# Seven products for the first token block's second projection, sums begun in the fifth half unit, last norm six half units later

## The chip, the cores and the metric

The kernel runs on one core of a Trainium2 chip. The metric is the device time of one execution in microseconds, lower is better; for the kernel before it is the median of three runs. The core has a matrix engine (PE, with its weight loads shown as PEld), three engines for elementwise work (DVE, ACT, POOL) and a queue that issues most DMAs (SP). Each engine works through its own queue in order, and waits for others by semaphores.

## What is computed

One transformer layer on 2 sequences of 1024 tokens with 256 features: self attention with 16 heads, cross attention to 154 context rows, and a gated feed-forward layer, each behind a layer norm and added to its input. All is fp32. The change lies in the last part:

```python
h = _layernorm(x, ln3_g, ln3_b)
p = h @ ff_w1 + ff_b1                      # 256 -> 2048
a, gate = (p[..., :D_FF], p[..., D_FF:])   # 1024 each
h = a * jax.nn.gelu(gate, approximate=False) @ ff_w2 + ff_b2   # 1024 -> 256
return h + x
```

## The kernel before

The program order of each engine is the order of the Python code (`tc.manual_schedule`). There are three stages: a loop over self attention, a loop over cross attention (variable `c`), and the last loop over half units (`k` from 0 to 63), which holds the gated layer. The change touches the last loop alone.

**Token blocks and units.** The 2048 tokens are cut into four blocks (`pair` 0 to 3) of 512 tokens, two halves of 256 each. Each block goes through eight units `n`, one for each slice of 128 of the 1024 hidden features. A unit has two half units: `gate_first(n)` at k = 2n and `gate_second(n)` at k = 2n + 1. The first projection is done in the manner of Strassen and Winograd: seven products of 256 columns in place of eight, with sums of weights and of tokens prepared by POOL (`weight_sums`, `token_sums`) and sums of results taken by DVE. An even half unit has four products on PE, since `gate_last(n - 1)` puts the seventh of the unit before in its middle; an odd one has three. POOL multiplies the two halves by their gates: L1081 (second half, emitted in the odd half unit) and L1090 (first half, emitted in the even half unit after, by `gate_last`). The results are the tiles `u`; the second half of block 0 lies in the old tile `kT`.

**Second projection.** When `gate_last` has done a block's last unit, it puts that block's products into the list `sums`, and the loop takes them from there by `sum_slot`, so block 0's products run beside block 1's units, from k = 16 on. Blocks 1 to 3 go through `partial`: seven products for each of two token halves, each of four matrix products with 128 columns, into the tiles `pf` (L1161). The seven need sums of weights (`column_sums`, four POOL instructions of 128x512, L1128, once) and sums of the gated values (`row_sums`, four POOL instructions of 128x256 for each of four pairs of slices, L1140 to L1143). `store` adds the results to `x` on DVE (L1170), five additions for each token half, and sends the finished token tiles on SP. Block 0 does the plain form: eight matrix products of 256 columns for each of four token tiles (L1200), one addition each (L1210), two products in every half unit.

**What else stands in the loop.** The last cross attention values are weighed at k = 0 and k = 3 (`poc`, L932), and the four last output pieces of cross attention (`py_ca`, L467) run at k = 4 to 6. At k = 7 `norm_beside("ff", B - 1)` queues the norm of the second sequence: from there each odd half unit runs one of seven steps, which together hold the statistics of two tiles on DVE (L240, L241), variance and power of the pair before on POOL (L246, L250), the factor `off` on DVE (L256) and the normalization of the pair before that on POOL (L267), then the transposes on PE (L280) and the scaling on ACT (L295). Token sums for the next block come at k = 8, 24, 40. From k = 13 on every third half unit lets POOL add the output bias to one token tile of `x` (L320); a DVE addition to the same tile that comes later in the program waits for it. `hold_sums` takes the buffer for column and row sums at k = 16; it is one of two buffers with the tag `pT`, and the one it takes held the transposed probabilities of cross attention until k = 3.

In the engines' queues the tile `own` of a unit holds its four intermediate results; DVE's L1060, L1062 and ACT's L1056 start a unit, L1076, L1079 and L1088 on DVE and L1074, L1080 on ACT finish it. PE's second product into a tile `pb` waits until L1060 has read the first.

Of the kernel before, what the change touches and what calls it, by code (L numbers as in the profile page):

```python
# [10 lines left out]
ALU = mybir.AluOpType  # L11
AX = mybir.AxisListType

P = 128
# [4 lines left out]
def tile_transformer_block(ctx: ExitStack, tc: tile.TileContext, a: dict, out: bass.AP):  # L19
    nc = tc.nc  # L20
# [3 lines left out]
    B, S, D = x.shape  # L24
# [7 lines left out]
    NT = S // P  # L32
    GT = 4
# [17 lines left out]
    NF = DF // P  # L51
    SH = GH // 2
    TF = 2
# [19 lines left out]
    def sum_tile(name):  # L73

        return ps_o.tile([P, HB], F32, tag="po", name=name)


    xt = {
        (b, g): const.tile([P, GT, D], F32, tag=f"x{b}{g}", name=f"x{b}{g}")
        for b in range(B) for g in range(NG)  # L80
    }
# [16 lines left out]
    for n in names:  # L98
        k = n_of[n]
# [8 lines left out]
    for n in names[:2]:  # L108
        for r0 in range(0, P, HR):
            (nc.scalar if n == names[0] else nc.sync).dma_start(  # L110
                out=cols[r0:r0 + HR, row_of[n]:row_of[n] + NH],
                in_=w[n].rearrange("(r p) -> p r", p=HR),
# [54 lines left out]
    for n in names[2:]:  # L167
        own = rows[row_of[n] - n_cols:row_of[n] - n_cols + n_of[n], :]
# [396 lines left out]
    def flush(queue):  # L565
        for fn in queue:
            fn()
        queue.clear()
# [188 lines left out]
    CG = [(t, min(TG, NT - t)) for t in range(0, NT, TG)]  # L757
# [204 lines left out]
    NPR = B * 2  # L962
    BT = S // 4
    FU = NPR * NF
    wsum, wh, ub, psum, pools = {}, {}, {}, {}, {}
# [98 lines left out]
    def biases(n):  # L1064
        c = row_of["ff_b1"] + n % NF
        return cols[:, c:c + 1], cols[:, c + NF:c + NF + 1]
# [16 lines left out]
    def gate_last(n):  # L1083

        pair, f = divmod(n, NF)
        pa, pb, pc, own = psum.pop(n)
        product(n, 4, pb, False)
        nc.vector.scalar_tensor_tensor(  # L1088
            own[:, 0, :], pb[:, :BT], biases(n)[0], own[:, 0, :], op0=ALU.add, op1=ALU.add)
        nc.gpsimd.tensor_tensor(ub[pair][0][:, f, :], own[:, 0, :], own[:, 3, :], ALU.mult)  # L1090
        if f == NF - 1:
            if pair:
                early, late = (1, 4, 2), (5, 6, 3, 7)
                if pair == NPR - 1:
                    sums.extend((pair, i, m) for m in early for i in range(TF))
                    sums.extend((pair, i, m) for i in range(TF) for m in late)
                else:
                    sums.extend((pair, i, m) for i in range(TF) for m in early + late)
            else:
                sums.extend((pair, i, e) for i in range(2 * TF) for e in range(NF))  # L1100

    sums, summed = [], {}

# [18 lines left out]
    def quarter(odd, d):  # L1122
        return w2[:, odd::2, d * P:(d + 1) * P]

    def column_sums(n):

        t = half["t"]
        nc.gpsimd.tensor_tensor(*[  # L1128
            lambda: (t[5], quarter(0, 1), quarter(0, 0)),
            lambda: (t[6], quarter(1, 1), t[5]),  # L1130
            lambda: (t[4], quarter(1, 0), t[6]),
            lambda: (t[7], quarter(1, 1), quarter(0, 1)),
        ][n](), ALU.subtract)

    def row_sums(pair, c):

        s = {i: own[:, c, :] for i, own in half["s"][pair % 2].items()}
        (a11, a12), (a21, a22) = ([ub[pair][j][:, 2 * c + e, :] for e in range(2)] for j in range(2))
        tt = nc.gpsimd.tensor_tensor
        tt(s[5], a21, a22, ALU.add)  # L1140
        tt(s[6], s[5], a11, ALU.subtract)
        tt(s[3], a12, s[6], ALU.subtract)
        tt(a21, a11, a21, ALU.subtract)  # L1143

    def partial(pair, i, m):

        if m == 1:
            bank = mm_tile if pair == NPR - 1 and i else sum_tile
            summed[pair, i] = [bank(f"pf{pair}_{i}_{r}") for r in range(2)]
        into, own = summed[pair, i]  # L1150
        at = {2: 0, 3: 1, 4: 2, 5: 3}.get(m)
        region = own[:, (m != 1) * P:][:, :P] if at is None else into[:, at * P:(at + 1) * P]
        token = slice(i * P, (i + 1) * P)
        for c in range(NF // 2):
            lhs = {
                1: lambda: ub[pair][0][:, 2 * c, token], 2: lambda: ub[pair][0][:, 2 * c + 1, token],
                4: lambda: ub[pair][1][:, 2 * c + 1, token], 7: lambda: ub[pair][1][:, 2 * c, token],
            }.get(m, lambda: half["s"][pair % 2][m][:, c, token])()
            rhs = {1: (0, 0), 2: (1, 0), 3: (1, 1)}.get(m)
            rhs = half["t"][m][:, c, :] if rhs is None else quarter(*rhs)[:, c, :]  # L1160
            nc.tensor.matmul(  # L1161
                region, lhsT=lhs, rhs=rhs, start=(c == 0 and m != 7), stop=(c == NF // 2 - 1),
                skip_group_check=True)
        if m in (2, 4, 5):
            return None
        b, g = divmod(pair, NG)
        xs = xt[b, g].rearrange("p (j i) (d k) -> p i j d k", i=TF, k=P)[:, i]

        def plus(x, y):
            nc.vector.tensor_tensor(x, y, x, ALU.add)  # L1170

        def send(j, queue):
            t = 2 * TF * pair % NT + j * TF + i
            queue.dma_start(out=out[b, t * P:(t + 1) * P, :], in_=xt[b, g][:, j * TF + i, :])

        def store():
            if m == 1:
                plus(xs, region.unsqueeze(1).unsqueeze(1).broadcast_to([P, 2, 2, P]))
            elif m == 6:
                plus(xs[:, 0, 1], region)  # L1180
            elif m == 3:
                plus(xs, into.rearrange("p (j d k) -> p j d k", j=2, d=2))
                plus(xs[:, 0, 1], into[:, 3 * P:4 * P])
                send(0, nc.sync)
            else:
                plus(xs[:, 1], region.unsqueeze(1).broadcast_to([P, 2, P]))
                send(1, nc.scalar if pair == NPR - 1 and i else nc.sync)

        return store

    def sum_slot():

        pair, i, f = sums.pop(0)
        if pair:
            return partial(pair, i, f)
        if f == 0:
            summed[pair] = sum_tile(f"pf{pair}_{i}")
        own = summed[pair]
        j, e = divmod(i, TF)
        nc.tensor.matmul(  # L1200
            own[:, :D], lhsT=ub[pair][j][:, f, e * P:(e + 1) * P], rhs=w2[:, f, :],
            start=(f == 0), stop=(f == NF - 1),
        )
        if f < NF - 1:
            return None
        b, t = divmod(pair * 2 * TF + i, NT)

        def store():
            xs = xt[b, t // GT][:, t % GT, :]
            nc.vector.tensor_tensor(xs, own[:, :D], xs, ALU.add)  # L1210
            nc.sync.dma_start(out=out[b, t * P:(t + 1) * P, :], in_=xs)

        return store


    with tc.manual_schedule():
# [11 lines left out]
        own = [ps_s.tile([P, 2, HB], F32, tag="s", name=f"first_{r}") for r in range(2)]  # L1228
# [88 lines left out]
        for c in range(CA):  # L1317
# [5 lines left out]
            if c == SH:  # L1323
                out_pieces("sa", B - 1, NQ - 1, out_order("sa"))
                w1, w2, parts = hold_gated()
# [27 lines left out]
            if n == 0 and ui > 1:  # L1353
                own, between = cross_values(ui - 2, [mm_tile] * 2 + [sum_tile] * 2)
# [54 lines left out]
        for k in range(2 * FU):  # L1409
            c = CA + k  # L1410
            weighed = {0: [part_tile] * 3 + [sum_tile], 3: [part_tile] * 2 + [sum_tile] * 2}.get(k)
            flush(adds)
            if k == 0:
                for copies in cross_values(NU - 2, weighed):
                    copies()
            (gate_second if k % 2 else gate_first)(k // 2)
            flush(stores)
            flush(lates)
            if k == 2 * len(CG) + 1:
                norm_beside("ff", B - 1)  # L1420
            if k == 0:
                load_out("ca", B - 1, NQ - 1)
            cross_drain(c)
            if k == len(CG):
                for copies in cross_values(NU - 1, weighed):
                    copies()
                out_pieces("ca", B - 1, NQ - 1, out_order("ca"))
            if k % (2 * NF) == NF and k < 2 * FU - 2 * NF:
                token_sums(k // (2 * NF) + 1)
            for _ in range(min(2 if k < 4 * NF else 1, len(sums))):  # L1430
                run(sum_slot)
            flush(stores)
            run_work(0 if k <= len(CG) else 1 + k % 2, k % 2)
            if later and k > 12 and k % 3 == 1:
                later.pop(0)()
            if k == 2 * NF:
                hold_sums()
            if k in (2 * NF + 2, 2 * NF + 4, 2 * NF + 8, 2 * NF + 10):
                column_sums((k - 2 * NF) // 3)
            pair, at = divmod(k - 5, 2 * NF)  # L1440
            if pair > 0 and at % 4 == 0:
                row_sums(pair, at // 4)
# [38 lines left out]
```

## Time and profile before

| | us |
|---|---|
| median of three runs | 1078.48 (1077.67 to 1078.64) |
| profiled execution, its own time | 1078.65 |
| span of that execution | 1076.9 |
| POOL busy over the span | 765.4 |
| DVE busy over the span | 875.2 |

The span is what the trace of the profiled execution covers; 1.75 us of its time lie around it. Rows of a timeline give start and length in us, engine, line, operation, output and inputs, the number of instructions merged, and in brackets the idle time ahead of it with what ended it. Rows of windows give the busy time of each engine in a stretch.

### The profile page before, as it was taken

Reading aid. Unit: us, or ns where it says so; the run is one execution under the profiler, and the core shown is the slowest. Engines: PE = TensorE matmul, PEld = TensorE weight load, DVE = VectorE, ACT = ScalarE, POOL = GpSimd, SP = SyncE. Lnnn points to the kernel's source line nnn. Section 1 sums busy time; section 2 is a strip of 40 time slices with the busy share of each in tenths; the row PEclk is TensorE's granted clock in tenths of the full one; section 3 lists DMA queues with packets and bytes.
Section 4 is the critical chain, followed back from the end, with each engine's and each line's share of the span. In section 5 each row is a group of like instructions: output and inputs, shape, how many; then the busy total and the mean of one; then the engine's idle time right before and its main releaser. Section 6 shows DMA issues by size and latency. Waiting matters only on the chain.

```text
span 1076.9 us, 45967 instructions
## 1 busy us (share of the span) xinstructions
PE 1065.6 (99%) x19060; PEld 712.3 (66%) x19060; DVE 875.2 (81%) x1283; ACT 651.0 (60%) x2081; POOL 765.4 (71%) x1600
## 2 busy tenths in 40 slices
PE   8999999999999999999999999999999999999998
PEld 6545657567565565566665655567766677788998
DVE  5789999998989989999989998978766777654554
ACT  5666767667666666666776666666566555242221
POOL 2677777778777787777777777768665687488774
PEclk9999999999999999999999999999999999999999
DMA  3232122111111111211211211135323221000000
GB/s 95 63 91 63 46 47 46 33 43 30 41 40 33 43 43 29 53 43 24 53 24 33 53 24 38 24 103 131 97 57 83 68 58 41 1 10 11 21 11 30
DMA packets 99234, 50.56 MB, mean 47 GB/s; under 512 B 30218, under 2 KB 97810, under 8 KB 99026
## 3 DMA queue, kind: packets, MB, share of 16 engines
q1 hardware_dynamic: 97698, 46.96, 18.0%
q8 instruction: 150, 2.46, 1.0%
q10 hardware_dynamic: 1328, 0.66, 0.2%
q14 instruction: 58, 0.48, 0.1%
HBM read 35.25 MB, written 3.41 MB: 36 GB/s over the span
## 4 chain that ended last, share of the span: by engine, by line
PE 91%; POOL 3%; DVE 2%; DMA 1%; ACT 1%; issue 1%; SPq 1%; DVEq 0%; POOLq 0%; ACTq 0%
PE s L493 19%; PE po L547 19%; PE py_sa L467 5%; PE py_ca L467 5%; PE pv_sa L393 5%; PE pq_ca L362 5%; PE pq_sa L362 5%; PE pk_sa L362 5%; PE sc L867 4%; PE poc L932 4%; PE pb L1037 3%; PE pf L1161 3%; PE pa L1037 2%; PE pc L1037 2%; PE pf L1200 1%; DMA st<-st 1%
## 5 line engine op out<-in xcount | busy, mean ns | idle before, releaser
L613 POOL TENSOR_SCALAR p<-p,rd,ee 128x512 f32<-128x512 f32 x508 | 387.4, 773 | 91.4 <-DVE rd L605 88.1
L508 ACT ACTIVATE p<-s,st 128x512 f32<-128x512 f32 x512 | 345.9, 687 | 175.5 <-DVE st L502 169.7
L502 DVE TENSOR_REDUCE st<-s 128x2 f32<-128x1024 f32 x256 | 308.8, 1207 | 51.1 <-issue 20.4
L640 DVE STREAM_TRANSPOSE pT<-p 128x1024 f32<-128x1024 f32 x256 | 302.4, 1219 | 1.5 <-POOL p L613 1.5
L493 PE MATMUL s<-k_sa,q_sa 64*32 64x512 f32 x4096 | 256.1, 591 | 2.4 <-ACT p L508 1.6
L547 PE MATMUL po<-pT,v_sa 64*32 64x256 f32 x8192 | 239.5, 376 | 0.9 <-ACT p L885 0.9
L547 PEld LDWEIGHTS po<-pT,v_sa 64*32 64x32 f32 x8192 | 177.5, 106 | 71.4 <-issue 26.2
L493 PEld LDWEIGHTS s<-k_sa,q_sa 64*32 64x32 f32 x4096 | 83.5, 106 | 101.0 <-issue 52.7
L885 ACT ACTIVATE p<-sc,neg 128x154 f32<-128x154 f32 x256 | 96.9, 401 | 74.9 <-DVE rden L893 74.4
L896 POOL TENSOR_SCALAR p<-p,rden 128x154 f32<-128x154 f32 x256 | 97.4, 402 | 61.7 <-DVE rden L893 61.2
L508 ACT ACTIVATION_READ_ACCUMULATOR p<-s,st 128x1 f32 x512 | 103.4, 202 | 0.0
L526 POOL TENSOR_TENSOR dd<-st 128x8 f32<-128x8 f32 x128 | 25.9, 202 | 73.5 <-DMA st<-st 69.7
L872 DVE TENSOR_REDUCE neg<-sc 128x6 f32<-128x924 f32 (+1 forms) x48 | 48.0, 1000 | 31.0 <-PE sc L867 30.9
L393 PEld LDWEIGHTS pv_sa<-sa_wv,hT_ln 64*128 64x128 f32 x1024 | 58.5, 188 | 14.2 <-issue 9.2
L393 PE MATMUL pv_sa<-sa_wv,hT_ln 64*128 64x128 f32 x1024 | 61.7, 275 | 0.0
L467 PE MATMUL py_ca<-ca_wo,o_ca 128*128 128x256 f32 x256 | 60.8, 385 | 0.0
L467 PE MATMUL py_sa<-sa_wo,o_sa 128*128 128x256 f32 x256 | 59.8, 386 | 0.0
L467 PEld LDWEIGHTS py_sa<-sa_wo,o_sa 128*128 128x128 f32 x256 | 47.2, 190 | 18.0 <-ACT v_sa L402 5.9
L362 PE MATMUL pq_ca<-hT_ln,ca_wq 64*128 64x512 f32 (+1 forms) x352 | 58.2, 589 | 0.0
L362 PE MATMUL pk_sa<-hT_ln,sa_wk 64*32 64x512 f32 x960 | 57.1, 590 | 0.0
L362 PE MATMUL pq_sa<-hT_ln,sa_wq 64*32 64x512 f32 (+1 forms) x976 | 56.7, 586 | 0.0
L885 ACT ACTIVATION_READ_ACCUMULATOR p<-sc,neg 128x1 f32 x256 | 55.3, 216 | 0.0
(132 smaller groups left out, 1442.6 us busy)
## 6 DMA issues: line engine op xcount, KB each, us to landing
v_sa<-v_sa SPq DMA_DIRECT2D x32, 256.0 KB, 3.8
st<-st SPq DMA_DIRECT2D x510, 1.0 KB, 1.8
v_ca<-vd SPq DMA_DIRECT2D x32, 160.0 KB, 3.1
sa_wq<-in_L_xattn_sa_wq_dram SPq DMA_DIRECT2D x32, 128.0 KB, 3.2
sa_wk<-in_L_xattn_sa_wk_dram SPq DMA_DIRECT2D x32, 128.0 KB, 3.2
sa_wv<-in_L_xattn_sa_wv_dram SPq DMA_DIRECT2D x32, 128.0 KB, 3.2
ca_wq<-in_L_xattn_ca_wq_dram SPq DMA_DIRECT2D x32, 128.0 KB, 3.4
wf<-in_L_xattn_ff_w_dram SPq DMA_DIRECT2D x12, 256.0 KB, 5.3
```

The costliest lines, as they stand in the source:

```text
L362: nc.tensor.matmul(pq[r][f:f + m, at:at + n], lhsT=wt[own, c, f:f + m], rhs=h[own, c, t0:t0 + n], start=(c == 0), stop=(c == NH - 1), tile ...
L393: nc.tensor.matmul(pv[r][:, i * P:(i + 1) * P], lhsT=h[own, c, i * P:(i + 1) * P], rhs=wt[own, c, :], start=(c == 0), stop=(c == NH - 1), ...
L467: nc.tensor.matmul(py[:, e * D:(e + 1) * D], lhsT=o[:, i, (t + e) * P:(t + e + 1) * P], rhs=wo[kind, b, g][:, i, :], start=(i == 0), stop= ...
L493: nc.tensor.matmul(sc[a4 * KB:(a4 + 1) * KB, j, :], lhsT=q[r, c:c + KB], rhs=k[r, h * HB:(h + 1) * HB], start=True, stop=True, tile_positi ...
L502: nc.vector.tensor_reduce(st[:, 0, 0, i, :], sc, AX.X, ALU.max, negate=True)
L508: nc.scalar.activation(pr[:, j, :], sc[:, j, :], AF.Exp, bias=st[:, 0, 0, i, j:j + 1], accum_out=st[:, 0, 1, i, j:j + 1],)
L547: nc.tensor.matmul(po[a2][d:d + KB, :QH // 2], lhsT=v[r, t, e, d:d + KB], rhs=pT[r, d // DH * NK + n, :], start=(t == 0 and e == 0), stop= ...
L613: nc.gpsimd.tensor_scalar(pr[:, j, :], pr[:, j, :], v["rd"][:, c:c + 1], v["ee"][:, 0, c:c + 1], op0=ALU.mult, op1=ALU.mult,)
L640: nc.vector.transpose(halves[h][:, :, c:c + KB], slot[p]["members"][i].rearrange("p j (n k) -> p (j n) k", k=KB))
L885: nc.scalar.activation(pr_[:, j, i, :T], sc[:, j, i * T:(i + 1) * T], AF.Exp, bias=neg[:, j, i:i + 1], accum_out=den[:, j, i:i + 1],)
L896: nc.gpsimd.tensor_scalar(pr_[:, j, i, :T], pr_[:, j, i, :T], rden[:, j, i:i + 1], 1.0, op0=ALU.mult, op1=ALU.mult,)
L1037: nc.tensor.matmul(into[:, :BT], lhsT=lhs, rhs=wh[pair][i], start=first, stop=True, skip_group_check=True)
```

## The change

Block 0's second projection goes through `partial` as well. So its sums stand in `sums` as 14 entries in place of 32, and one entry is taken in each half unit, from k = 16 to 29. The column sums move from k = 18, 20, 24, 26 to k = 4, 5, 6, 7, with `hold_sums` at k = 4 ahead of them. Row sums for block 0 are new, at k = 9, 11, 14 and 17; those of the other blocks stay where they were. The last norm is queued at k = 13 in place of k = 7. The branch of `sum_slot` for the plain form goes away.

```diff
         if f == NF - 1:
-            if pair:
-                early, late = (1, 4, 2), (5, 6, 3, 7)
-                if pair == NPR - 1:
...
-                else:
-                    sums.extend((pair, i, m) for i in range(TF) for m in early + late)
+            early, late = (1, 4, 2), (5, 6, 3, 7)
+            if pair == NPR - 1:
...
             else:
-                sums.extend((pair, i, e) for i in range(2 * TF) for e in range(NF))
+                sums.extend((pair, i, m) for i in range(TF) for m in early + late)
...
     def sum_slot():
 
-        pair, i, f = sums.pop(0)
-        if pair:
-            return partial(pair, i, f)
...
-        nc.tensor.matmul(
-            own[:, :D], lhsT=ub[pair][j][:, f, e * P:(e + 1) * P], rhs=w2[:, f, :],
-            start=(f == 0), stop=(f == NF - 1),
-        )
...
-        return store
+        return partial(*sums.pop(0))
...
-            if k == 2 * len(CG) + 1:
+            if k == 4 * len(CG) + 1:
                 norm_beside("ff", B - 1)
...
-            for _ in range(min(2 if k < 4 * NF else 1, len(sums))):
+            for _ in range(min(1, len(sums))):
                 run(sum_slot)
...
-            if k == 2 * NF:
+            if k == len(CG) + 1:
                 hold_sums()
-            if k in (2 * NF + 2, 2 * NF + 4, 2 * NF + 8, 2 * NF + 10):
-                column_sums((k - 2 * NF) // 3)
+            if len(CG) < k < NF:
+                column_sums(k - len(CG) - 1)
+            if k in (NF + 1, NF + 3, 2 * NF - 2, 2 * NF + 1):
+                row_sums(0, (k - NF) // 3)
             pair, at = divmod(k - 5, 2 * NF)
             if pair > 0 and at % 4 == 0:
                 row_sums(pair, at // 4)
```

Here `NF` is 8 and `len(CG)` is 3. The changed source is 21 lines shorter, so its line numbers from here on differ: L1158 there is L1161 here, L1167 is L1170, L1137 to L1140 are L1140 to L1143, L1125 is L1128.

More of the change, by code (lines that the diff above doesn't have):

```diff
@@ L1091, in gate_last @@
         if f == NF - 1:
-            if pair:
-                early, late = (1, 4, 2), (5, 6, 3, 7)
-                if pair == NPR - 1:
-                    sums.extend((pair, i, m) for m in early for i in range(TF))
-                    sums.extend((pair, i, m) for i in range(TF) for m in late)
-                else:
-                    sums.extend((pair, i, m) for i in range(TF) for m in early + late)
+            early, late = (1, 4, 2), (5, 6, 3, 7)
+            if pair == NPR - 1:
+                sums.extend((pair, i, m) for m in early for i in range(TF))
+                sums.extend((pair, i, m) for i in range(TF) for m in late)
             else:
-                sums.extend((pair, i, e) for i in range(2 * TF) for e in range(NF))
+                sums.extend((pair, i, m) for i in range(TF) for m in early + late)
     sums, summed = [], {}
@@ L1191, in sum_slot @@
     def sum_slot():
-        pair, i, f = sums.pop(0)
-        if pair:
-            return partial(pair, i, f)
[L1196 to L1200, printed above, removed]
-            own[:, :D], lhsT=ub[pair][j][:, f, e * P:(e + 1) * P], rhs=w2[:, f, :],
-            start=(f == 0), stop=(f == NF - 1),
-        )
[L1204 to L1211, printed above, removed]
-        return store
+        return partial(*sums.pop(0))
     with tc.manual_schedule():
```

## The prediction

> **What bounds the kernel now.** I read the page first, then the busy time by windows over the last stage, then the timelines of PE, POOL and DVE there.
>
> ```profile
> span 1076.9 us, 45967 instructions
> ...
> PE 1065.6 (99%) x19060; PEld 712.3 (66%) x19060; DVE 875.2 (81%) x1283; ACT 651.0 (60%) x2081; POOL 765.4 (71%) x1600
> ...
> PE 91%; POOL 3%; DVE 2%; DMA 1%; ACT 1%; issue 1%; SPq 1%; DVEq 0%; POOLq 0%; ACTq 0%
> ```
>
> PE is the bound over the whole span: 99% busy, 91% of the chain. The change lies in the last loop, so the stage has to be read by itself:
>
> ```profile
> 925.00:930.00 5.00, 5.00 (x24) 4.39 (x24) 2.65 (x5) 0.51 (x2) 1.46 (x2) 1.00 0.00 0
> ...
> 935.00:940.00 5.00, 4.86 (x23) 3.85 (x22) 4.09 (x12) 1.56 (x5) 4.77 (x9) 1.00 0.00 0
> 940.00:945.00 5.00, 4.35 (x22) 3.22 (x21) 4.42 (x15) 2.13 (x6) 4.59 (x9) 1.00 0.00 0
> ...
> 950.00:955.00 5.00, 5.00 (x27) 4.41 (x26) 2.78 (x6) 2.28 (x5) 5.00 (x10) 1.00 0.00 2
> ...
> 960.00:965.00 5.00, 5.00 (x25) 4.41 (x24) 2.20 (x6) 1.36 (x3) 3.37 (x5) 1.00 0.00 0
> ```
>
> The columns after the window's length are PE, PEld, DVE, ACT and POOL, each with its count, then PE's clock (1.00 here). From 935 on POOL is as full as PE: 4.77, 4.59 and 5.00 us of 5, while the normalization and the token sums are in its queue. There PE drops to 4.35. Before 930 POOL has room (1.46 of 5). So here two engines are near the bound at once, and this is the stretch in which POOL gets more work.
>
> ```profile
> 916.77 2.41 PE L932 MATMUL poc<-pT_ca,v_ca 32*64 32x256 f32 x80
> ...
> 932.17 0.59 PE L1037 MATMUL pa<-hT_ln,wf 128*128 128x256 f32 x2
> ...
> 933.90 0.59 PE L1037 MATMUL pa<-hT_ln,wf 128*128 128x256 f32 x2
> 934.63 0.70 PE L1037 MATMUL pb<-hT_ln,wf 128*128 128x256 f32 x2
> ...
> 941.84 0.70 PE L1037 MATMUL pb<-hT_ln,wf 128*128 128x256 f32 x2 [0.49 <-DVE own L1060]
> ...
> 947.34 0.60 PE L1037 MATMUL pa<-hT_ln,wf 128*128 128x256 f32 x2
> ...
> 949.07 1.03 PE L1200 MATMUL pf<-wf,u 128*128 128x256 f32 x4
> 949.94 0.59 PE L1037 MATMUL pa<-hT_ln,wf 128*128 128x256 f32 x2
> ...
> 952.10 0.60 PE L280 MATMUL ph_ln<-ident,xn_ln 128*128 128x128 f32 x4
> 952.53 0.60 PE L1037 MATMUL pa<-hT_ln,wf 128*128 128x256 f32 x2
> ...
> 986.21 0.59 PE L1037 MATMUL pa<-hT_ln,wf 128*128 128x256 f32 x2
> ...
> 987.94 1.05 PE L1161 MATMUL pf<-wf,u 128*128 128x128 f32 x8
> 988.83 0.60 PE L1037 MATMUL pa<-hT_ln,wf 128*128 128x256 f32 x2
> ```
>
> An fp32 product stands as two records. Half unit k=8 begins at 932.17, k=9 at 933.90, k=16 at 947.34, k=32 at 986.21. The four products of an even half unit take 1.73 (947.34 to 949.07), one takes 0.4325, the three of an odd one 1.30, a pair 3.03. Two wide sum products (x4) take 0.87, four narrow ones (x8) 0.89 or 0.2225 each, the transposes of one norm step 0.43 (952.10 to 952.53).
>
> **Part 1, PE.** Removed: 4 token tiles x 8 wide products = 32 x 0.4325 = 13.84. Added: 2 token halves x 7 x 4 = 56 narrow ones x 0.2225 = 12.46. PE saves **1.38 us**, if nothing waits.
>
> **Part 2, what stalls today.** From k=8 to k=32 PE has 12 pairs (36.36), 32 wide products (13.84) and four norm steps (1.72): 51.92. It takes 986.21 - 932.17 = 54.04, so **2.12 us** are stalls. They are the norm's: its statistics stand in DVE's queue ahead of the additions that PE waits for (pb at 934.63 is 0.30 late, at 941.84 it names DVE). Moving the norm takes them from here.
>
> **Part 3, POOL's queue after the change.**
>
> ```profile
> 933.42 0.72 POOL L1081 TENSOR_TENSOR kT<-own 128x256 f32<-128x256 f32 x1 [3.64 <-ACT own L1080]
> 934.32 0.73 POOL L1090 TENSOR_TENSOR u<-own 128x256 f32<-128x256 f32 x1 [0.18 <-DVE own L1088]
> 935.01 0.73 POOL L1020 TENSOR_TENSOR hs<-hT_ln 128x256 f32<-128x256 f32 x1
> ...
> 937.87 0.73 POOL L1081 TENSOR_TENSOR kT<-own 128x256 f32<-128x256 f32 x1
> 938.67 0.19 POOL L246 TENSOR_SCALAR var_ln<-mv_ln 128x2 f32<-128x2 f32 x1
> 938.95 0.71 POOL L250 TENSOR_TENSOR rstd_ln<-var_ln,power 128x2 f32<-128x2 f32 x1
> 939.62 0.73 POOL L1090 TENSOR_TENSOR u<-own 128x256 f32<-128x256 f32 x1
> ...
> 942.09 1.10 POOL L267 TENSOR_SCALAR xn_ln<-x,rstd_ln,off_ln 128x256 f32<-128x256 f32 x2
> 943.15 0.73 POOL L1090 TENSOR_TENSOR u<-own 128x256 f32<-128x256 f32 x1
> ...
> 946.87 0.73 POOL L320 TENSOR_TENSOR x<-x,ff_b 128x256 f32<-128x256 f32 x1
> 947.55 0.74 POOL L1090 TENSOR_TENSOR u<-own 128x256 f32<-128x256 f32 x1
> ...
> 963.54 0.72 POOL L1140 TENSOR_TENSOR wx<-u 128x256 f32<-128x256 f32 x1
> ...
> 966.52 0.73 POOL L1090 TENSOR_TENSOR u<-own 128x256 f32<-128x256 f32 x1
> ...
> 972.39 1.27 POOL L1128 TENSOR_TENSOR wx<-wf,wx 128x512 f32<-128x512 f32 x1
> 973.61 0.73 POOL L1081 TENSOR_TENSOR u<-own 128x256 f32<-128x256 f32 x1
> ```
>
> Start to start: a gate product or bias addition 0.69, token sums 2.86 (935.01 to 937.87), variance with power 0.95 (938.67 to 939.62), a normalized pair of tiles 1.06 (942.09 to 943.15), row sums 2.98 (963.54 to 966.52), a column sum 1.22 (972.39 to 973.61). Added are four row sums, 11.92 us, at k=9, 11, 14, 17. The column sums (4.88) leave k=18 to 26 for k=4 to 7; the first three fall into the room before 930, and their buffer is free once the last reading of the old probabilities ends (916.77 + 2.41). They cost nothing; without that room they would add 1.22 each to what follows. The fourth stands at k=7, behind the product at 933.42. From there the queue never empties; its order is the changed program's, "u6e" being the product of unit 6 for the even half:
>
> 933.42 u3o, column sum, u3e, token sums (to 938.88), u4o, row sums 0, u4e, u5o, row sums 1 (946.91), u5e, u6o, bias; **u6e ends 949.71**; row sums 2 (952.65); **u7o ends 953.38**; variance, u7e (954.98), bias, u8o, variance, normalize (958.37); **first row sum of the last group ends 959.10**, the group's last step 961.35; u8e, u9o, variance, normalize (**second tile ends 964.78**), bias, u9e, u10o, variance, normalize (968.82), row sums of the second block (971.80), u10e; **bias of tile 3 ends 973.22**.
>
> The Trainium skill, "Perfetto Trace Analysis", section GPSIMD Engine Instruction, says that spans of this engine are unreliable and to time it from start to start; the trace agrees (the addition at 946.87 lasts 0.73, the next starts 0.68 later). By the spans the queue would end about 0.7 later and the time would be 1082.9.
>
> **Part 4, PE against that queue.** k=8 still begins at 932.17. Eight half units bring it to 944.29; the first statistics (now k=13) stall once as at 934.63, 0.30, so k=16 begins at 944.59. The rest adds 0.05 from POOL's end to PE's start, the 0.06 between DVE's end (below) and pb at 941.84 being the nearest row.
> - k=16: 1.73 and three narrow products, 946.99. The fourth needs u6e, 949.76: **2.77**. Done 949.98.
> - k=17: 1.30 + 0.67 = 951.95; the fourth needs u7o, 953.43: **1.48**. Done 953.65. k=18 waits for nothing: 956.27.
> - k=19: 958.24; the fourth needs the row sum, 959.15: **0.91**. With the transposes, 959.80.
> - k=20, 21: 964.61; the second transpose needs the tile that ends 964.78: **0.12**. Then k=22 to 24 run to 973.02.
> - k=25: its second product needs L1060 on DVE. DVE's queue there is: addition of the first sum to tiles 1 and 3, which needs tile 3's bias from POOL; the norm's off; L1088; L1060.
>
> ```profile
> 940.64 0.41 DVE L256 SCALAR_TENSOR_TENSOR off_ln<-mv_ln,rstd_ln 128x2 f32<-128x2 f32 x1
> 940.98 0.47 DVE L1088 SCALAR_TENSOR_TENSOR own<-pb,cols,own 128x256 f32<-128x256 f32 x1
> 941.37 0.41 DVE L1060 TENSOR_TENSOR own<-pb,own 128x256 f32<-128x256 f32 x1
> ```
> ```profile
> L1170 DVE TENSOR_TENSOR x<-pf,x 128x512 f32<-128x512 f32 x12 | 8.3, 692 | 6.2 <-PE pf L1161 6.2
> ```
>
> From 973.28: 0.69 + 0.34 + 0.39 + 0.41 = 975.11, to PE 975.17. PE is there at 973.45: **1.72**.
>
> Stalls after: 0.30 + 2.77 + 1.48 + 0.91 + 0.12 + 1.72 = **7.30**. Behind it POOL's next product that PE needs is at k=32, and it has drained by then: from 973.18 nine gate products and biases (6.21), one normalize (1.06), token sums (2.86), two groups of row sums (5.96) stand ahead of u14e, which so ends near 990.0; it is asked for at 989.97 + 2.40.
>
> **Part 5, the rest.** DVE gets ten additions to x in place of four: at most 10 x 0.69 = 6.9 us over 14 half units, beside 2.20 of 5 busy; hidden but for the wait above. Four 128 KB stores still leave on SP, from two half units later to two earlier; nothing in the loop waits for them. Cost 0, and if SP were late, 0 too until the last store of the program.
>
> **Sum.** -1.38 - 2.12 + 7.30 = **+3.80 us** on the profiled execution's 1078.65 (span 1076.9): 1082.45. That run is 0.17 above the median of 1078.48, so the forecast for the median is **1082.2**. Bounds: PE's position at k=25 is set by about 40 us of back-to-back POOL; 2% on that is 0.8 either way, and the waits could be 0.6 dearer if each restart costs what pb's did at 941.84. Own range 1081.0 to 1083.6.
>
> **Rivals.**
> 1. *PE alone decides, faster.* POOL would have to keep ahead, so that the saving of 1.38 and the 2.12 of norm stalls both remain: 1078.48 - 3.50 = **1075.0**. It speaks for it that PE is 91% of the chain and that the second block does the same work with PE at 5.00. Against it: in the first block norm, token sums and row sums stand together, and 11.92 us are added where POOL has 0.0 to 0.4 us of 5 free. It decides at k=16: fourth product of the first sum without a wait. The Trainium skill, "Perfetto Trace Analysis", section Identifying the Most-Contended Engine, says to shorten the engine with the highest occupancy first, which over the span is PE; its section Optimization Strategy adds that the busiest engine can change from regime to regime, and the windows agree with that (POOL 5.00 of 5 from 950 to 955).
> 2. *The backlog costs less, no change.* If DVE's wait for the bias does not pass on to PE (1.72) and the first waits are some 1.0 shorter because POOL gets a little ahead before 933, +1.1: **1079.6**. No row shows the bias or the products of k=7 ready earlier, so both halves have to be hoped for.
> 3. *The backlog lasts.* POOL still holds token sums (2.86) and the second block's row sums (2.98) when PE needs the next block's products: another stall of about 3: **1085.2**. Against it, the 2.4 us of room that Part 4 finds at k=32.
> 4. *The narrow products give nothing.* If one cost half of a wide one plus another 0.025, PE saves 0 and the sum is +5.2, **1083.7**; the 0.89 of the row at 987.94 speaks against it.
>
> **How the numbers follow.** Forecast 0.72, rival 1 0.10, rival 2 0.11, rival 3 0.05, rival 4 0.02. About 0.2%, or 2.2 us, is what a measurement can tell from no change: 1076.3 to 1080.6. Slower: forecast, 3, 4 = 0.79; same: 0.11; faster 0.10. The range 1079.2 to 1084.6 takes in the forecast's own and most of rivals 2 and 4, and leaves out rivals 1 and 3.
>
> **What would show it.** In the changed profile: POOL near 5.00 of 5 from 935 to past 970; PE waiting in the sum line for L1090 (about 2.8), L1081 (1.5) and the first row sum (0.9) between 946 and 960, and a pb behind L1060 near 975; the first products of the third token block, today at 986.21, near 990; from there the same rhythm as before, and a span near 1080.7. The prediction is wrong if POOL shows gaps between 935 and 960, or if PE reaches the first sum after u6e is done.

## The result and the profile after

| | us |
|---|---|
| changed kernel, median of five | 1082.70 (1081.82 to 1083.08) |
| kernel before beside it, median of five | 1078.48 (1077.67 to 1078.92) |
| ratio of the two, with its 95% interval | 1.0039 (1.0024 to 1.0054) |
| profiled execution of the changed kernel | 1081.82, span 1080.0 |

The change made the kernel slower by 4.2 us; the forecast was 1082.2. To see where the time went, PE's timeline is cut at the first product of some half units. That of k=0 stands between 909.29 and 911.48 in the profiled executions of this case, also where nothing ahead of it was changed, so the loop is counted from there: from the first product of k=0 (910.22 before, 909.47 after) to the end of the span (1076.9, 1080.0).

| stretch | before, us | after, us |
|---|---|---|
| k=0 to 8 | 21.95 | 21.95 |
| k=8 to 16 | 15.17 | 12.49 |
| k=16 to 32 | 38.87 | 45.50 |
| k=32 to the end | 90.69 | 90.59 |
| the loop | 166.68 | 170.53 |

The loop is 3.85 us longer; the sum of the prediction was 3.80. The medians differ by 4.22, and the interval of their ratio, 2.6 to 5.8 us, takes in both. All of the loop's difference lies in the stretch that the prediction named: 2.68 us are gained up to k=16 (the norm's stalls, and two of its four transpose steps of 0.43, which come later now), 6.63 are lost in the next sixteen half units, and from k=32 on the two run alike.

The windows of the changed kernel, with the same columns as before:

```profile
940.00:945.00 5.00, 4.87 (x24) 3.84 (x23) 4.18 (x13) 1.97 (x6) 4.77 (x8) 1.00 0.00 0
945.00:950.00 5.00, 2.51 (x14) 2.15 (x13) 1.82 (x7) 0.34 (x2) 4.92 (x8) 0.89 0.01 3
950.00:955.00 5.00, 5.00 (x24) 4.34 (x23) 3.55 (x10) 1.35 (x3) 4.75 (x9) 0.77 0.00 0
...
970.00:975.00 5.00, 3.78 (x22) 3.13 (x21) 1.81 (x5) 1.77 (x4) 4.64 (x9) 1.00 0.00 0
```

POOL is full (4.6 to 4.9 of 5) over the whole stretch, and it is PE that stands still: 2.51 of 5 from 945 to 950, 3.78 from 970 to 975. The granted clock, 1.00 in the windows around, falls to 0.89 and then 0.77. PE's own timeline shows the waits:

```profile
943.91 0.59 PE L1037 MATMUL pa<-hT_ln,wf 128*128 128x256 f32 x2
...
945.64 0.83 PE L1158 MATMUL pf<-wf,u 128*128 128x128 f32 x6
948.96 0.79 PE L1158 MATMUL pf<-wf,u 128*128 128x128 f32 x2 [2.49 <-POOL u L1090]
949.54 1.06 PE L1037 MATMUL pa<-hT_ln,wf 128*128 128x256 f32 x2
950.40 1.06 PE L1037 MATMUL pb<-hT_ln,wf 128*128 128x256 f32 x2
951.25 1.06 PE L1037 MATMUL pc<-hT_ln,w1s 128*128 128x256 f32 x2
952.11 1.16 PE L1158 MATMUL pf<-wx,kT 128*128 128x128 f32 x8
953.10 0.60 PE L1037 MATMUL pa<-hT_ln,wf 128*128 128x256 f32 x2
...
958.58 0.49 PE L1158 MATMUL pf<-wx 128*128 128x128 f32 x2 [0.73 <-POOL wx L1137]
...
974.47 0.70 PE L1037 MATMUL pb<-hT_ln,wf 128*128 128x256 f32 x2 [1.22 <-DVE own L1060]
```

The first sum (k=16) does three of its four products (x6) and waits 2.49 us for the fourth's input from POOL. At k=17, from 949.54, there is no wait in brackets: the products there start 0.86 apart and not 0.43. At k=19 POOL's row sum is late, at k=25 the addition L1060 on DVE. What held that addition up stands in DVE's queue, and POOL's queue shows what both engines waited for:

```profile
972.94 0.69 DVE L1167 TENSOR_TENSOR x<-pf,x 128x512 f32<-128x512 f32 x1 [3.60 <-POOL x L320]
973.54 0.15 DVE L256 SCALAR_TENSOR_TENSOR off_ln<-mv_ln,rstd_ln 128x2 f32<-128x2 f32 x1
973.61 0.48 DVE L1088 SCALAR_TENSOR_TENSOR own<-pb,cols,own 128x256 f32<-128x256 f32 x1
974.01 0.41 DVE L1060 TENSOR_TENSOR own<-pb,own 128x256 f32<-128x256 f32 x1
```

```profile
932.67 0.73 POOL L1081 TENSOR_TENSOR kT<-own 128x256 f32<-128x256 f32 x1 [2.42 <-ACT own L1080]
...
948.19 0.72 POOL L1090 TENSOR_TENSOR u<-own 128x256 f32<-128x256 f32 x1
...
951.84 0.72 POOL L1081 TENSOR_TENSOR kT<-own 128x256 f32<-128x256 f32 x1
952.65 0.19 POOL L246 TENSOR_SCALAR var_ln<-mv_ln 128x2 f32<-128x2 f32 x1
...
957.81 0.72 POOL L1137 TENSOR_TENSOR wx<-kT 128x256 f32<-128x256 f32 x1
...
972.18 0.72 POOL L320 TENSOR_TENSOR x<-x,ff_b 128x256 f32<-128x256 f32 x1
```

DVE waits 3.60 us for POOL's bias addition, then works off what is queued behind it. Of POOL's rows behind the one at 932.67, none up to 972.18 has an idle time in brackets: 40 us of work end to end.

### The profile page after: what moved, and what is told of

Its sections match the earlier page's. It is cut to its first block, busy times and chain, and to the rows that moved or that the text cites. A ratio compares the mean times of both kernels' runs of the same rounds, so it can differ in the third digit from the quotient of the medians.

```text
span 1080.0 us, 46089 instructions
## 1 busy us (share of the span) xinstructions
PE 1064.9 (99%) x19108; PEld 703.1 (65%) x19108; DVE 876.5 (81%) x1289; ACT 649.5 (60%) x2081; POOL 772.7 (72%) x1616
## 4 chain that ended last, share of the span: by engine, by line
PE 88%; POOL 5%; DVE 2%; ACT 1%; DMA 1%; issue 1%; SPq 1%; DVEq 0%; POOLq 0%; ACTq 0%
PE s L493 19%; PE po L547 19%; PE py_sa L467 5%; PE py_ca L467 5%; PE pv_sa L393 5%; PE pq_ca L362 5%; PE pq_sa L362 5%; PE pk_sa L362 5%; PE pf L1158 4%; PE sc L867 4%; PE poc L932 4%; PE pb L1037 3%; PE pa L1037 2%; PE pc L1037 2%; DMA st<-st 1%
## 5 line engine op out<-in xcount | busy, mean ns | idle before, releaser
L547 PEld LDWEIGHTS po<-pT,v_sa 64*32 64x32 f32 x8192 | 173.3, 106 | 75.2 <-issue 28.9
L493 PEld LDWEIGHTS s<-k_sa,q_sa 64*32 64x32 f32 x4096 | 79.5, 106 | 105.2 <-issue 58.4
```

Source lines behind the costliest of these rows:

```text
L493: nc.tensor.matmul(sc[a4 * KB:(a4 + 1) * KB, j, :], lhsT=q[r, c:c + KB], rhs=k[r, h * HB:(h + 1) * HB], start=True, stop=True, tile_positi ...
L547: nc.tensor.matmul(po[a2][d:d + KB, :QH // 2], lhsT=v[r, t, e, d:d + KB], rhs=pT[r, d // DH * NK + n, :], start=(t == 0 and e == 0), stop= ...
```

## The experiments

The loop's length is counted as above, from each run's own profile, and waits are the times in brackets there. Ratios are to the kernel before, measured beside each; its median was 1078.85 beside e1 to e4, 1077.96 beside e5 to e8 and 1078.29 beside e9 and e10, so the medians of different runs are compared by their ratios.

**e1, the norm alone.** The kernel before, with one edit:

```diff
-            if k == 2 * len(CG) + 1:
+            if k == 4 * len(CG) + 1:
                 norm_beside("ff", B - 1)
```

> The kernel before with one edit, the last norm queued at k=13. Theory (POOL's queue sets PE): block 0 stays plain, so POOL has room, and of the 2.12 us of norm stalls only those of the two steps ahead of k=16 stay, 0.3 to 0.6; about 1.6 us faster than before, 1076.9. Rival (the later norm itself costs): its transposes then stand beside the sums, POOL is late for them, and the time is 1079 or more.

Median 1077.13, ratio 0.9986 (0.9977 to 0.9994), loop 164.81, so 1.87 us shorter. The stretch from k=8 to 16 takes 12.49 as in the changed kernel, and PE's timeline names no wait for another engine in that stretch any more. The norm's move is a gain by itself; the loss comes from the seven products.

**e4, a dose of POOL.** The changed kernel with more work in POOL's queue: the first token sum is done three times, with the same result each time. The added line moves the source's numbers up by one, so L1021 here is L1020 above.

```diff
-        nc.gpsimd.tensor_tensor(t[:, 0, :], own[0][1], own[0][0], ALU.subtract)
+        for _ in range(3 if pair == 1 else 1):
+            nc.gpsimd.tensor_tensor(t[:, 0, :], own[0][1], own[0][0], ALU.subtract)
```

> The changed kernel with two more POOL instructions of 128x256 at k=8 (the first token sum done three times), 1.37 us ahead of everything PE waits for. Theory: POOL's queue is the path, so the time rises by the same 1.4 us, to 1084.1. Rival (POOL is off the path, the waits seen are slack of something else): 1082.7, unchanged.

Median 1083.95, ratio 1.0046 (1.0034 to 1.0059), loop 172.35: 1.82 us longer than the changed kernel's. From POOL's timeline of this run:

```profile
935.64 2.35 POOL L1021 TENSOR_TENSOR hs<-hT_ln 128x256 f32<-128x256 f32 x3
938.07 0.73 POOL L1022 TENSOR_TENSOR hs<-hT_ln,hs 128x256 f32<-128x256 f32 x1
```

The three take 2.43 where one took 0.82 (935.26 to 936.08 in the changed kernel): the dose was 1.6 and not 1.37. Each writes what the one before wrote. The row sums of the changed kernel show the same spacing, 0.80, where an instruction reads what the one ahead of it wrote, and 0.69 where it does not. The wait at k=16 grows by as much as the dose, from 2.49 to 4.14. By the profiles POOL's added time goes into the kernel's in full; the ratios alone, 1.0046 beside 1.0039, are too close to tell.

**e5, the clock.** The changed kernel with products on PE ahead of the first sum, whose result is not used:

```diff
+            if k == 2 * NF:
+                fill = mm_tile("fill")
+                for _ in range(6):
+                    nc.tensor.matmul(fill[:, :D], lhsT=w2[:, 0, :P], rhs=w2[:, 0, :], start=True, stop=True, skip_group_check=True)
             for _ in range(min(1, len(sums))):
```

> The changed kernel with six idle products of 256 columns on PE at k=16, ahead of the first sum, which fill most of its first wait (six times 0.43 of 2.49 us); their result is not used. Theory (POOL's queue): the granted clock stays at 1.00, but the sum at k=17 then waits some 1.5 us for POOL's u7o, which the slow products cover now; within 0.4 us of the changed kernel. Rival (the lowered clock behind the wait is a cost of its own): three products at full speed, 1.3 us faster than the changed kernel.

Median 1082.14, ratio 1.0039 (1.0025 to 1.0053), loop 170.51, against 170.53. PE's timeline:

```profile
946.26 2.75 PE L1410 MATMUL fill<-wf 128*128 128x256 f32 x12
...
949.93 0.60 PE L1037 MATMUL pa<-hT_ln,wf 128*128 128x256 f32 x2
950.36 0.59 PE L1037 MATMUL pb<-hT_ln,wf 128*128 128x256 f32 x2
...
953.26 0.49 PE L1158 MATMUL pf<-wx,kT 128*128 128x128 f32 x2 [1.20 <-POOL kT L1081]
```

With PE busy the clock stays at 1.00 in both windows from 945 to 955, the products at k=17 start 0.43 apart, and the wait of 1.20 that the slow clock had covered appears. In the changed kernel the lowered clock costs nothing of its own: POOL sets the end of k=17 either way.

**e6, the sums two half units later.**

```diff
-            for _ in range(min(1, len(sums))):
+            for _ in range(min(int(not 2 * NF <= k < 2 * NF + 2), len(sums))):
```

> The changed kernel with the sums begun at k=18 and not 16. Theory: the wait only moves. PE reaches the transposes at k=19 ahead of POOL's first normalized tiles (957.8) and waits there about 5 us, and 1 us at k=19's sum; within 0.7 us of the changed kernel. Rival (the sums stand too early, and the rest of POOL's queue is slack): the waits of k=16 and 17 go and the time falls by 2.5 to 4 us.

Median 1082.47, ratio 1.0045 (1.0031 to 1.0059), loop 170.92. The wait moved, as the theory had it, but to another place, k=19's second product. First PE's row, then DVE's:

```profile
957.16 1.22 PE L1037 MATMUL pb<-hT_ln,wf 128*128 128x256 f32 x2 [4.49 <-DVE own L1060]
```
```profile
955.70 0.67 DVE L256 SCALAR_TENSOR_TENSOR off_ln<-mv_ln,rstd_ln 128x2 f32<-128x2 f32 x1 [4.59 <-POOL rstd_ln L250]
```

The norm's factor `off` on DVE waits for POOL's power, and the addition that frees `pb` is queued behind it. The expectation had the transposes of that half unit as the first thing to stop PE; it is this DVE instruction, which stands ahead of them.

**e7, the norm back at k=7.** The reverse of e1's edit in the changed kernel.

> The changed kernel with the last norm queued at k=7 as before. Theory: four variances and two or more normalizations, some 5 us, get ahead of u6e in POOL's queue, the wait at k=16 grows to about 7 us and those behind it shrink, since the whole of the queue up to the bias at k=22 is much the same; 0 to 1.5 us slower than the changed kernel. Rival (moving the norm is a part of the loss): up to 1.5 us faster.

Median 1085.43, ratio 1.0070 (1.0056 to 1.0084), loop 173.98, 3.45 us longer than the changed kernel's: the sign as expected, the size more than double. PE's timeline shows a place that the expectation had left out:

```profile
946.06 1.44 PE L280 MATMUL ph_ln<-ident,xn_ln 128*128 128x128 f32 x4 [3.38 <-POOL xn_ln L267]
947.30 1.06 PE L1037 MATMUL pa<-hT_ln,wf 128*128 128x256 f32 x2
948.15 1.06 PE L1037 MATMUL pb<-hs,wf 128*128 128x256 f32 x2
...
959.75 0.33 PE L280 MATMUL ph_ln<-ident,xn_ln 128*128 128x128 f32 x1 [1.13 <-POOL xn_ln L267]
```

The transposes now stand at k=13 and stop PE before the sums do, and the clock falls to 0.54 in the window behind. The products then start 0.85 apart until 952.3. This half pace is not what costs the 3.45 us: POOL's rows have no idle time in brackets from 933.50 to 968.37, and at k=17 PE waits for POOL once more, 1.13 us at 959.75. Up to there POOL alone sets PE, whose transposes of k=13 and k=17 wait for normalizations that stand behind row sums in POOL's queue. What follows is that the later norm is a part that the seven products need.

**e2, the bias additions early.** The changed kernel with

```diff
-            if later and k > 12 and k % 3 == 1:
+            if later and (k < 9 or k % 3 == 1):
                 later.pop(0)()
```

> The changed kernel with the eight bias additions of the first sequence moved from every third half unit after 12 to k=1 to 8, where POOL has room. Theory: two of them leave the queue ahead of the first row sum (1.38 us), and DVE's wait for tile 3's bias, 1.2 to 1.7 us on PE, goes: about 2.8 us faster than the changed kernel, 1079.9. Rival (the narrow products or the lowered clock cost the time): 1082.7 as before the edit.

Median 1080.87, ratio 1.0017 (1.0008 to 1.0025), loop 168.98: 1.55 us shorter, against 2.8 expected. The wait at k=25 is gone. But the two additions of k=7 and 8 now stand in the queue ahead of `u6e`, where only that of k=13 had stood, and the wait at k=16 grew:

```profile
950.59 0.58 PE L1158 MATMUL pf<-wf,u 128*128 128x128 f32 x2 [3.17 <-POOL u L1090]
```

0.68 more than 2.49, one POOL instruction.

**e3, the token sums early too.** As e2, and

```diff
-            if k % (2 * NF) == NF and k < 2 * FU - 2 * NF:
+            if k == 2 or k % (2 * NF) == NF and NF < k < 2 * FU - 2 * NF:
                 token_sums(k // (2 * NF) + 1)
```

> As e2, and the second block's token sums (2.86 us of POOL) moved from k=8 to k=2. Theory: POOL keeps ahead of PE, all waits of k=16, 17, 19 and 25 go and the saving on PE remains: before - 1.38 - 2.12 + 0.6 = 1075.6, faster than both kernels. Rival (narrow products cost more than half of a wide one): 1079 or more.

Median 1077.76, ratio 0.9993 (0.9984 to 1.0002), loop 166.21. The expectation had left them out again: the two additions of k=7 and 8 are still in the queue, and PE waits 0.36, 1.21 and 0.22 us at k=16, 17 and 19. It is about as fast as the kernel before, and no more.

**e8, all of it before 930.** As e3, but two additions at a time for k below 9, so that all are done by k=4, and the column sums at k=4, 4, 5 and 6:

```diff
+            for _ in range(min(2 if k < 9 else int(k % 3 == 1), len(later))):
+                later.pop(0)()
...
+            for n in {4: (0, 1), 5: (2,), 6: (3,)}.get(k, ()):
+                column_sums(n)
```

> The changed kernel with POOL's work moved into its room before 930: the eight bias additions two at a time at k=1 to 4, the second block's token sums at k=2, the column sums at k=4, 4, 5, 6. Theory: 2.86 + 0.69 + 1.22 us leave the queue ahead of u6e, and 0.69 more ahead of the first row sum, so all waits of PE go but about 0.3 to 0.5: before - 1.38 - 2.12 + 0.5, 1075.9 where before is 1078.85. Rival (POOL's room before 930 is not real, since work there delays the cross attention's end): 1077.8 or more.

Median 1077.32, ratio 0.9989 (0.9980 to 0.9998), loop 165.20, 1.48 us shorter than before: half of the 2.95 that was expected. POOL's timeline has the reason:

```profile
934.20 0.73 POOL L1081 TENSOR_TENSOR kT<-own 128x256 f32<-128x256 f32 x1 [1.10 <-ACT own L1080]
934.88 0.73 POOL L1090 TENSOR_TENSOR u<-own 128x256 f32<-128x256 f32 x1
937.22 0.72 POOL L1081 TENSOR_TENSOR kT<-own 128x256 f32<-128x256 f32 x1 [1.61 <-ACT own L1080]
937.90 0.73 POOL L1137 TENSOR_TENSOR wx<-kT 128x256 f32<-128x256 f32 x1
```

With so much moved ahead POOL runs empty twice, 2.7 us, while the first row sums stand behind the product of k=9. What is taken out ahead of a gap does not bring forward what stands behind it, and PE still waits 0.87 and 0.21 us.

**e9, the first row sums into that gap.** As e8, and

```diff
-            if k in (NF + 1, NF + 3, 2 * NF - 2, 2 * NF + 1):
-                row_sums(0, (k - NF) // 3)
+            for c4 in {NF - 1: (0,), NF + 3: (1,), 2 * NF - 2: (2,), 2 * NF + 1: (3,)}.get(k, ()):
+                row_sums(0, c4)
```

> As e8, with block 0's first row sums at k=7 and not 9; in e8 POOL is idle there (2.7 us between 933 and 937.3) and PE still waits 0.87 and 0.21 us for it at k=17 and 19. Theory: that idle time takes the 2.98 us, those two waits go, and the loop from the first product of k=0 to the end of the span shrinks from e8's 165.20 by about 1.2 us, to 164.0; 1076.1 where before is 1078.85, and faster than e1, the best plain form (164.81). Rival (the narrow products save nothing once POOL keeps up): no faster than e1, 164.8 or more.

Median 1075.41, ratio 0.9974 (0.9965 to 0.9983), loop 163.88. PE's windows now stay full through what was the bad stretch:

```profile
945.00:950.00 5.00, 5.00 (x32) 4.61 (x32) 4.61 (x15) 1.89 (x5) 4.67 (x8) 1.00 0.01 3
950.00:955.00 5.00, 5.00 (x34) 4.50 (x33) 3.24 (x11) 1.04 (x3) 4.69 (x9) 1.00 0.00 2
```

This version beats both kernels, by 0.26% the one before. Its loop is 0.93 us shorter than that of e1, the best with the plain form; the intervals of the two ratios overlap, so that this comparison rests on the profiles.

**e10, the row sums on DVE.**

```diff
-        tt = nc.gpsimd.tensor_tensor
+        tt = (nc.gpsimd if pair else nc.vector).tensor_tensor
```

> The changed kernel with block 0's row sums on DVE in place of POOL. Theory: 5.96 us leave POOL's queue ahead of u6e and 11.9 ahead of the bias of tile 3, so PE's waits for POOL go; but four DVE instructions (some 1.5 us) then stand ahead of the additions that PE waits for at four places, where the norm's statistics of 1.08 us cost 0.30: 0.7 each, 3 in all. Loop 166.68 - 3.5 + 0.3 + 3.0 = 166.5, the time of before. Rival (the two engines hinder each other where both read SBUF, so POOL's instructions lengthen): 169 or more.

Median 1082.04, ratio 1.0032 (1.0020 to 1.0044), loop 171.02: the rival's side. PE no longer waits for POOL; it waits for DVE, 2.21 us at k=11 and 1.38 at k=16. The row of PE, then those of DVE and of POOL, at the first group:

```profile
940.48 1.19 PE L1037 MATMUL pb<-hT_ln,wf 128*128 128x256 f32 x2 [2.21 <-DVE own L1060]
```
```profile
938.76 0.94 DVE L1140 TENSOR_TENSOR kT<-u,kT 128x256 f32<-128x256 f32 x1
...
944.57 0.41 DVE L1140 TENSOR_TENSOR kT<-u,kT 128x256 f32<-128x256 f32 x1
```
```profile
938.52 0.90 POOL L1022 TENSOR_TENSOR hT_ln<-hT_ln 128x256 f32<-128x256 f32 x1
939.38 0.90 POOL L1023 TENSOR_TENSOR hs<-hT_ln,hs 128x256 f32<-128x256 f32 x1
940.25 0.72 POOL L1081 TENSOR_TENSOR kT<-own 128x256 f32<-128x256 f32 x1
```

The same DVE instruction takes 0.94 us beside a busy POOL and 0.41 beside an idle one, and POOL's token sums go from 0.73 in the changed kernel to 0.90. How the loss divides between this lengthening, the lowered clock behind the wait (0.66 in the window from 940 to 945) and the four instructions' own time on DVE was not taken apart.

## Why the prediction was right, point by point

**PE's saving (1.38).** The narrow sums take 0.89 each as costed. Between e9 and e1, the two that hardly wait, 0.93 us of it is seen in the loop; e9 keeps small losses at k=19 and 21 that add up to 0.46 (38.86 from k=16 to 32, against 38.40 for the work: 24.22 for the first projection, 12.46 for the sums, 1.72 for the transposes), and 0.93 + 0.46 is 1.39.

**The norm's stalls (2.12).** e1 gained 1.87 and kept 0.37 (12.49 against 12.12 from k=8 to 16), 2.24 in all.

**POOL's queue.** Counted from the start of `u3o`, the prediction had the ends that PE waits for at 16.29 (`u6e`), 19.96 (`u7o`), 25.68 (the row sum) and 39.80 (the bias of tile 3). The trace of after has 16.24, 19.89, 25.86 and 40.23: off by 0.43 us after 40. The order was right step by step, and so were the steps but one: variance and power, 0.95, begin 0.80 after the instruction ahead of them (951.84 to 952.65) and not 0.69. The rows of before show it too, 937.87 to 938.67. Four such steps make 0.44, two ahead of the row sum and two behind it.

The prediction's other sum, by spans, came out wrong: with the spans of its own rows the queue ends 0.44 later than by starts (40.24), not 0.7. By spans `u7o` would end at 20.22, and it ended at 19.89, so that the last ends agree, 40.24 and 40.23, is chance. That end of `u7o` agrees with the Trainium skill's rule to time this engine from start to start ("Perfetto Trace Analysis", GPSIMD Engine Instruction).

**PE's waits.** What each half unit took beyond its work, predicted and measured:

| | predicted | measured |
|---|---|---|
| k=13 to 15, statistics | 0.30 | 0.37 |
| k=16, `u6e` | 2.77 | 3.01 |
| k=17, `u7o` | 1.48 | 1.37 |
| k=19, row sum | 0.91 | 1.01 |
| k=21, normalized tile | 0.12 | 0.20 |
| k=25, bias by way of DVE | 1.72 | 1.49 |
| sum | 7.30 | 7.45 |

Two lines are right in size and not in kind. At k=16 the wait is 2.65 of the 3.01; the rest is the fourth product at half pace, 0.58 in place of 0.22. At k=17 PE did not wait, it ran at half pace, and e5 shows that the wait is there once the pace is not. The prediction had no lowered clock at all. That this cost it nothing is luck in part: the slow products happened to fit into a wait for POOL that it had right.

At k=25 two errors met. POOL's bias came 0.43 later than predicted, but PE did as well, by 0.39 (counted from k=8). DVE's chain behind it took 1.52 and not 1.89, mostly since L256 took 0.07 (973.54 to 973.61) and not 0.34. So the close sum, 7.45 against 7.30, hides small misses of both signs. The last step, from 1082.28 by its terms to the stated 1082.2, is a rounding.

**The rivals.** That PE alone decides fell at its own test, the fourth product of the first sum, which waited 2.49 us. The Trainium skill's rule to optimize the engine with the highest occupancy first ("Perfetto Trace Analysis", Identifying the Most-Contended Engine) led to the right gain only once POOL kept up, in e9. The windows from 945 to 950 show POOL at 4.92 and PE at 2.51 of 5; the Trainium skill's remark that the most-contended engine can change over time ("Perfetto Trace Analysis", Optimization Strategy) agrees with that. That the backlog costs less is ruled out by the waits: 7.45 where it had 4.6, and PE's row at 974.47 shows that DVE's wait for the bias is passed on. That it lasts longer is ruled out by the last stretch, 90.59 beside 90.69. That the narrow products give nothing is ruled out by their 0.89 and by e9. What the prediction did not see is how easily POOL's work could be moved: the room before 930 was in its own windows.

## What to carry to other kernels

Before work is taken from the engine with 99% of the span, lay the queue of the engine that pays for it end to end over that stretch, from the last moment it was idle; here 12 us more of POOL cost some 7 us of PE's time for 1.38 us saved. Then look ahead of the stretch for idle time in that same queue: moving work there turned a loss of 0.39% into a gain of 0.26%. Count what stands in an in-order queue ahead of each wait, and check for gaps, since work removed ahead of a gap gains nothing behind it (e8).

## What the hardware showed that was not expected

**PE's clock falls after a wait of a few microseconds.** In the changed kernel a wait of 2.49 us was followed by products 0.86 apart in place of 0.43, for about 3 us, with a mean granted clock of 0.77 in that window. The windows behind the waits in e4 (4.14), e2 (3.17) and e10 (2.21) show 0.66, in e6 (4.49) 0.70 and in e7 (3.38) 0.54; in e7 the half pace lasted some 6 us. After the waits of up to 1.38 us in e3, e5, e8 and e10 the windows show 1.00. The Trainium skill, "TensorE: Matmul & The Clock Gate", section HAM oscillation, gives gaps above some 3.4 us as those to avoid. The halved pace agrees with that section of the Trainium skill, but here 2.2 to 2.5 us were enough. In these few waits the limit lies between 1.38 and 2.21 us; the runs do not say what else it depends on.

**DVE and POOL slow each other on SBUF operands.** In this kernel PE's results lie in PSUM and the other tiles in SBUF. e10's rows above are DVE's additions with both inputs in SBUF; those that read one input from PSUM show no such thing (L1060 takes 0.41 beside a busy POOL, at 974.01 in the changed kernel). The Trainium skill, "SBUF — State Buffer", section SBUF: two separate sides, says that the two engines share a port pair which a DVE instruction with two SBUF inputs takes against a POOL instruction that reads SBUF, the other being blocked. Here both lengthen, by 0.53 and 0.17 us in the rows above. That fits a shared port; which of the two waited for it, no run here takes apart.
